# A planned graph-network kernel: the first batch's layer 0 chunk by chunk, first transfers ranked by need, its diagonal blocks on VectorE, and a new planned cost of a power

## The chip, the cores and the metric

One core of one Trainium2 chip. The metric is the device time of one execution in microseconds (us), over 32 batches. "Before" and "after" are the two kernels; each experiment was run on one chip together with runs of the kernel before, and is compared with those. A difference between runs of two sessions is marked as such; the kernel before had medians of 2319.06 to 2320.55 us in the sessions of the experiments.

## The reference

Four pre-normalized graph layers on x (32 batches of 512 nodes by 128 features), each with the batch's dense 512 by 512 adjacency:

```python
# layer 0: normalized adjacency with self loops
h = jnp.maximum(_layernorm(x, axis=-1), 0.0)
def _L0_gnn_ref(X, adj, W, b):
    XW = jnp.einsum('bnf,fo->bno', X, W)
    adj = adj + jnp.eye(adj.shape[1], dtype=adj.dtype)[None]
    d = jnp.sum(adj, axis=-1)
    r = d ** (-0.5)
    adj = adj * r[:, :, None] * r[:, None, :]
    y = jnp.einsum('bnm,bmo->bno', adj, XW) + b
    return jax.nn.leaky_relu(y, negative_slope=0.01)
x = x + _L0_gnn_ref(h, adj, ...)
# layers 1 to 3: layernorm, relu, then
#   1: two aggregations (adj and its transpose) of ELU features, tanh update
#   2: four inner layers, each with two aggregations by l2-normalized adjacency
#   3: one aggregation and a GRU-like gate
# ... each ends in x = x + layer(h, adj)
```

Every layer starts with a layernorm, and the l2 normalization needs inverse norms too, so each batch computes inverse square roots five times (four of them for the layernorms); here they are powers with exponent -0.5, done by GpSimd.

## The kernel before

The program is not written in the order in which it runs. Each operation is entered with an estimated cost, and a planner simulates the engines and fixes the order on each engine (and the buffer slots) before the program is built. Batches overlap: while TensorE works on one batch, the chains of the next are woven in between. Costs therefore change nothing on the chip by themselves; they change which instruction stands ahead of which.

Names in the views: v, sc and nb are the steps of the layernorm chain (variances, their power, the bias), h is its result; f is the tanh that ends an inner layer; blk is a transpose on VectorE, on the way of a tensor out to DRAM and back in another layout; f4r is such a turned tensor, read back from DRAM as turn_f4r; sd, rep and agg are operands of TensorE's products (ps_...). *Idle products* are products of the identity, put in where TensorE is planned to have nothing to do.

```python
PERIOD = 30.0
class Plan:
    SIGNAL = {"PE": 0.2, "DVE": 0.13, "ACT": 0.14, "POOL": 0.0, ...}
    RATE, ALONE, TRANSFER, ISSUE = 400.0, 175.0, 1.5, 0.45   # model of a transfer
    def op(self, engine, us, emit, reads=(), writes=(), kb=0.0, rank=None, later=0.0):
        ...
        if kb:
            o.us = max(self.ISSUE, kb / self.RATE)
            o.land = self.TRANSFER + kb / self.ALONE - o.us
    def order(self):
        ...
            due = o.batch * PERIOD if o.batch < B - 1 else (B - 2) * PERIOD + ENDING
            o.key = (due - o.tail + o.later if o.rank is None else o.rank - 1e6, i)
        ...  # events: each engine takes the ready operation with the lowest key
    def kept_warm(self, done, product, begin):
        ...  # where TensorE is planned idle for over SHORT us, n idle products are put in

def t_pow(n):                 # planned cost of a power over n columns
    return 0.9 + 0.1 * n

def normed(xin, out_tag, extra=None):          # layernorm and relu, every layer
    ... mv = moments(xin, v8)                  # VectorE
    if extra: extra(v8); n = 2 * NC            # layer 0: row sums of the adjacency too
    op("POOL", t_pow(n), lambda: nc.gpsimd.tensor_tensor(inv..., op=ALU.pow), ...)
    ... # layer 0: one VectorE multiply of two 4-column operands (sc)
    op("DVE", 0.08, ... nb = -mean * inv ...)
    for c in range(NC):
        op("ACT", t_act(D, 2), ... h = Relu(x * inv + nb) ...)

def degree(v8):                                # row sums, ScalarE
    for c in range(NC):
        op("ACT", 0.73, lambda c=c: nc.scalar.activation(
            sq.ap(), a.ap()[:, c, :], AF.Copy, accum_out=stat.ap()[:, c:c + 1]), ...)
hr, inv0 = normed(xt, "h", degree)

def own(k, n):                                 # diagonal blocks of aT plus identity
    nc.gpsimd.tensor_tensor(diag.ap()[:, k:k + n, :], blocks, ident..., op=ALU.add)
n = NC if b else 1                             # 4 of 128 columns first, then 1 of 512
```

## Time and profile before

Median of 3 runs: 2320.03 us.

The prediction below shows the page, the steady stretches and the head's timeline. The form whose time it takes for a row sum is VectorE's tensor_tensor of 128x512 f32, 687 to 689 ns in this trace (aT and a by rows, L739). One view also belongs here: what each engine waits for, summed over the run. First the head of TensorE's list in the kernel before (columns: total us, times, longest):

```profile
PE ps_agg L326 <- ACT f L768: 3.8, 5, 1.1
```

and the line of ScalarE's list that belongs to the layernorm chain:

```profile
ACT h L478 <- DVE nb L474: 144.1, 73, 8.2
```

TensorE waits for almost nothing. ScalarE waits 144 us for nb, the last VectorE step of a chain VectorE, GpSimd power, VectorE, ScalarE. That is harmless as long as what stands *behind* h in ScalarE's order is not needed yet. One such thing is f, the tanh that ends an inner layer and that TensorE needs for its next products.

### The profile page before, as it was taken

How to read it: one execution, taken by the hardware profiler on the slowest of the kernel's cores; microseconds unless marked ns; L12 is line 12 of the kernel's file. 1: busy time of each engine (PE TensorE's matmuls, PEld its weight loads, DVE VectorE, ACT ScalarE, POOL GpSimd, SP SyncE). 2: the span in 40 equal slices, each digit the busy share in tenths (PEclk: the TensorE clock that was granted, in tenths of full speed). 3: DMA queues.
4: the chain of work that ended last, by engine and by line, in shares of the span. 5: the costliest groups of instructions: out<-in, count | busy, mean ns of one | idle time of the engine just before them, and what ended most of it. 6: DMA issues, size and time to landing. Idle time of an engine off the chain costs nothing.

```text
span 2319.2 us, 28279 instructions
## 1 busy us (share of the span) xinstructions
PE 2301.0 (99%) x9682; PEld 1446.3 (62%) x9682; DVE 1530.8 (66%) x4132; ACT 946.4 (41%) x2018; POOL 262.6 (11%) x218
## 2 busy tenths in 40 slices
PE   9999999999999999999999999999999999999998
PEld 7656666666666566666666666666666666656665
DVE  5655666666667676676766676766766666767655
ACT  7323344334443344443344433444433444334412
POOL 3001101011111011010111101110101111101101
PEclk9999999999999999999999999999999999999999
DMA  7102332233222232222332322322223322223200
GB/s 261 46 10 64 105 94 75 81 101 107 76 91 82 82 109 81 87 79 86 105 100 83 91 82 82 109 81 88 78 86 105 107 76 91 82 82 105 77 6 27
DMA packets 133054, 200.82 MB, mean 87 GB/s; under 512 B 18992, under 2 KB 79920, under 8 KB 132912
## 3 DMA queue, kind: packets, MB, share of 16 engines
q1 hardware_dynamic: 132624, 198.90, 28.0%
q8 instruction: 76, 1.25, 0.2%
q14 instruction: 66, 0.54, 0.1%
q10 hardware_dynamic: 288, 0.13, 0.0%
HBM read 160.05 MB, written 38.93 MB: 86 GB/s over the span
## 4 chain that ended last, share of the span: by engine, by line
PE 91%; DMA 3%; DVE 3%; ACT 2%; POOL 1%; SPq 0%; issue 0%; DVEq 0%; ACTq 0%; POOLq 0%
PE ps_agg L326 61%; PE ps_seven L597 11%; PE ps_sd L326 9%; PE ps_upd L326 4%; PE ps_gate L326 2%; PE ps_msg L326 1%; DMA f4r<-turn_f4r 1%; PE ps_node L326 1%; PE ps_lin L326 1%; ACT h L478 1%; DMA turn_f4r<-blk 1%; POOL sc L466 1%; SPq L496 0%; ACT f L768 0%; DVE bn L450 0%
## 5 line engine op out<-in xcount | busy, mean ns | idle before, releaser
L326 PE MATMUL ps_agg<-aT,sd 128*128 128x512 f32 x1024 | 510.5, 594 | 0.1
L326 PE MATMUL ps_agg<-a,sd 128*128 128x512 f32 x1024 | 482.4, 592 | 0.0
L466 POOL TENSOR_TENSOR sc<-v,neg_half 128x4 f32<-128x4 f32 (+1 forms) x128 | 157.8, 1233 | 1638.6 <-DVE v L453 1361.8
L326 PEld LDWEIGHTS ps_agg<-a,sd 128*128 128x128 f32 x1024 | 184.6, 190 | 182.8 <-issue 178.4
L326 PE MATMUL ps_agg<-f,w_sb 128*128 128x512 f32 x448 | 229.6, 594 | 3.9 <-ACT f L768 3.8
L326 PEld LDWEIGHTS ps_agg<-aT,sd 128*128 128x128 f32 x1024 | 177.7, 191 | 83.0 <-issue 66.7
L326 PE MATMUL ps_sd<-w_sb,f 128*128 128x256 f32 x768 | 217.4, 380 | 0.5 <-ACT f L768 0.4
L478 ACT ACTIVATE h<-xr,nb,sc 128x128 f32<-128x128 f32 x384 | 158.2, 482 | 136.4 <-DVE nb L474 136.3
L597 PEld LDWEIGHTS ps_seven<-t_sb,s 128*128 128x128 f32 x1128 | 161.6, 191 | 78.1 <-issue 69.3
L326 PEld LDWEIGHTS ps_sd<-w_sb,f 128*128 128x128 f32 x768 | 136.6, 191 | 95.2 <-issue 76.5
L597 PE MATMUL ps_seven<-t_sb,s 128*128 128x128 f32 x1128 | 168.1, 275 | 0.0
L735 ACT COPY rows<-spaced 128x1024 f32<-128x1024 f32 x32 | 66.1, 2064 | 164.9 <-DMA spaced<-bounce 164.9
L326 PE MATMUL ps_agg<-aT,rep 128*128 128x512 f32 x256 | 131.3, 596 | 2.1 <-DVE rep L693 2.1
L326 PE MATMUL ps_agg<-a,rep 128*128 128x512 f32 x256 | 131.3, 596 | 0.0
L768 ACT ACTIVATE f<-ps_agg,cf_sb 128x512 f32<-128x512 f32 x128 | 87.2, 682 | 98.8 <-PE ps_agg L326 98.8
L326 PE MATMUL ps_agg<-aT,msg 128*128 128x512 f32 x256 | 124.9, 592 | 0.0
L487 DVE STREAM_TRANSPOSE blk<-f 128x512 f32<-128x512 f32 x29 | 20.6, 711 | 144.2 <-ACT f L768 144.2
L326 PE MATMUL ps_agg<-aT,h 128*128 128x256 f32 (+2 forms) x384 | 99.3, 381 | 0.2 <-ACT h L478 0.2
L597 PEld LDWEIGHTS ps_seven<-w_sb,f 128*128 128x128 f32 x512 | 75.9, 191 | 35.4 <-issue 27.7
L739 DVE TENSOR_TENSOR aT<-aT,rows 128x512 f32<-128x512 f32 x128 | 87.9, 687 | 14.7 <-PE ps_agg L326 14.6
L553 DVE TENSOR_TENSOR sd<-ps_sd,rf_sb 128x512 f32<-128x512 f32 x128 | 86.9, 679 | 15.5 <-PE ps_sd L326 15.4
L739 DVE TENSOR_TENSOR a<-a,rows 128x512 f32<-128x512 f32 x128 | 88.1, 689 | 13.6 <-PE ps_agg L326 13.5
(144 smaller groups left out, 3817.3 us busy)
## 6 DMA issues: line engine op xcount, KB each, us to landing
aT<-in_adjt SPq DMA_DIRECT2D x124, 512.0 KB, 5.2
a<-in_adj SPq DMA_DIRECT2D x62, 512.0 KB, 5.2
turn_turned<-blk SPq DMA_DIRECT2D x348, 64.0 KB, 1.8
turned<-turn_turned SPq DMA_DIRECT2D x87, 256.0 KB, 2.6
spaced<-bounce SPq DMA_DIRECT2D x32, 512.0 KB, 4.0
x<-in_x SPq DMA_DIRECT2D x32, 256.0 KB, 2.8
out<-xo SPq DMA_DIRECT2D x30, 256.0 KB, 2.0
turn_f4r<-blk SPq DMA_DIRECT2D x116, 64.0 KB, 1.8
```

The lines of the kernel that those rows point to most:

```text
L326: op("PE", t_mm(n), lambda: nc.tensor.matmul(out_of(ps.ap()), lhs(), rhs(), start=start, stop=stop), reads, [ps], later=later)
L466: op("POOL", t_pow(n), lambda: nc.gpsimd.tensor_tensor(inv.ap()[:, :n], v8.ap()[:, :n], neg_half[:, :n], op=ALU.pow), [v8, NH], [(inv, {0})])
L478: op("ACT", t_act(D, 2), lambda c=c: nc.scalar.activation(h.ap()[:, c, :], xin.ap()[:, c, :], AF.Relu, bias=nb.ap()[:, c:c + 1], scale=inv ...
L487: op("DVE", t_tt(N), lambda: nc.vector.transpose(blk.ap().rearrange("p b (c r) -> p c b r", c=NC), m.ap().rearrange("p c (b s) -> p c b s" ...
L553: op("DVE", t_tt(N), lambda ps=ps, h=h: nc.vector.tensor_add(sd.ap()[:, 2 * h:2 * h + 2, :], ps.ap().rearrange("p (j v) -> p j v", j=2), s ...
L597: op("PE", t_mm(D), lambda j=j: nc.tensor.matmul(ps.ap()[:, k * H + j * D:k * H + (j + 1) * D], lhs()[:, j * P:(j + 1) * P], rhs(), start= ...
L735: op("ACT", t_act(2 * N), lambda: nc.scalar.copy(rows.ap().rearrange("p s (c n) -> p (s c) n", c=NC), spaced.ap().rearrange("p n k -> p k ...
L739: op("DVE", t_tt(N), lambda m=m, c=c, s=s: nc.vector.tensor_mul(m.ap()[:, c, :], m.ap()[:, c, :], rows.ap()[:, s, :]), [(m, {c}), rows], [ ...
L768: op("ACT", t_act(N, 1), lambda ps=ps, i=i, f_new=f_new: nc.scalar.activation(f_new.ap(), ps.ap(), AF.Tanh, bias=cf_sb[:, i:i + 1]), [ps, ...
```

## The change

The intent: the layer-0 chain of the first batch shall follow the adjacency chunk by chunk, so that TensorE starts its first aggregation sooner. Four parts, cut to the core:

```diff
+OWN = 1
+FIRST = ["x0", "a0", "c", "raw0", "aT0", "w1", "r1", "raw2", "raw3"]
     def t_pow(n):
-        return 0.9 + 0.1 * n
+        return 0.35 + 0.157 * n
+    def first(name):
+        return FIRST.index(name) if name in FIRST else None
-        op("SP", 0.5, lambda: nc.sync.dma_start(c_sb, bcol), [], [CS], kb=9, rank=2)
+        op("SP", 0.5, lambda: nc.sync.dma_start(c_sb, bcol), [], [CS], kb=9, rank=first("c"))
 ... (the other transfers likewise)
+        def normed_by_chunk(xin, out_tag):
+            mv = moments(xin, v8)
+            op("POOL", t_pow(NC), ... pow of the 4 variances ...)
+            for c in range(NC):
+                op("DVE", t_tt(N), ... tensor_reduce(stat[:, c], a[:, c, :], AX.X, ALU.add) ...)
+                op("DVE", 0.08, ... v8 = stat + 1 ...)
+                op("POOL", t_pow(1), ... pow of one column ...)
+                op("DVE", 0.08, ... multiply the two inverses ...)
+                op("DVE", 0.08, ... nb ...)
+                op("ACT", t_act(D, 2), ... h of this chunk ...)
-        hr, inv0 = normed(xt, "h", degree)
+        hr, inv0 = normed_by_chunk(xt, "h") if b < 1 else normed(xt, "h", degree)
-            nc.gpsimd.tensor_tensor(diag..., op=ALU.add)
+            own_engine.tensor_tensor(diag..., op=ALU.add)
+        own_engine, own_name = (nc.vector, "DVE") if b < OWN else (nc.gpsimd, "POOL")
```

Three parts touch the first batch alone. The cost of a power touches the plan of all 32.

More of the change, by code (lines that the diff above doesn't have):

```diff
@@ L341, in setup @@
         op("POOL", 0.2, lambda: nc.gpsimd.memset(neg_half, -0.5), [], [NH])
-        first = W_L2[0][0]
+        first_l2 = W_L2[0][0]
         def spread(lo, hi, to=None):
@@ L351, in setup @@
             r_sb[:, :D], bass.AP(tensor=brow.tensor, offset=brow.offset, ap=[[0, P], [1, D]])), [], [(RS, {0})], kb=64)
-        op("SP", 0.5, lambda: nc.sync.dma_start(c_sb, bcol), [], [CS], kb=9, rank=2)
-        op("SP", 0.5, lambda: nc.sync.dma_start(w_sb[:, D:first], w[:, D:first]), [], [(W1, {1})], kb=(first - D) / 2, rank=5)
-        op("SP", 0.5, spread(D, R_L3_MSG), [], [(RS, {1})], kb=(R_L3_MSG - D) / 2, rank=5)
+        op("SP", 0.5, lambda: nc.sync.dma_start(c_sb, bcol), [], [CS], kb=9, rank=first("c"))
+        op("SP", 0.5, lambda: nc.sync.dma_start(w_sb[:, D:first_l2], w[:, D:first_l2]), [], [(W1, {1})], kb=(first_l2 - D) / 2, rank=first("w1"))
+        op("SP", 0.5, spread(D, R_L3_MSG), [], [(RS, {1})], kb=(R_L3_MSG - D) / 2, rank=first("r1"))
         op("SP", 0.5, spread(R_L3_MSG, R_COLS), [], [(RS, {2})], kb=(R_COLS - R_L3_MSG) / 2)
@@ L364, in setup @@
             op("SP", 0.5, lambda buf=buf, lo=lo, hi=hi: nc.sync.dma_start(
-                buf.ap().rearrange("p c n -> p (c n)")[:, :hi - lo], raw[:, lo:hi]), [], [buf], kb=(hi - lo) / 2, rank=3 if i == 0 else 6)
+                buf.ap().rearrange("p c n -> p (c n)")[:, :hi - lo], raw[:, lo:hi]), [], [buf], kb=(hi - lo) / 2, rank=first(f"raw{i}"))
             raws += [(buf, lo)] * (2 if i == 0 else 1)
-        op("SP", 0.5, lambda: nc.sync.dma_start(w_sb[:, W_L3_MSG:], w[:, first:]), [], [W3], kb=(W_COLS - W_L3_MSG) / 2)
+        op("SP", 0.5, lambda: nc.sync.dma_start(w_sb[:, W_L3_MSG:], w[:, first_l2:]), [], [W3], kb=(W_COLS - W_L3_MSG) / 2)
         def block(i, col):
@@ L435, in load @@
         def load(dst, src, kb, rank):
+            rank = first(f"{rank}{b}")
             n = NC // pieces
@@ L440, in load @@
                 op("SP", 0.4, lambda s=s: nc.sync.dma_start(dst.ap()[:, s, :], src[:, s, :]),
-                   [], [(dst, set(range(NC)[s]))], kb=kb / pieces, rank=None if b else rank)
-        op("SP", 0.4, lambda: nc.sync.dma_start(xt.ap(), x[b]), [], [xt], kb=256, rank=None if b else 0)
-        load(a, adj[b], 1024, 1)
-        load(aT, adjt[b], 1024, 4)
+                   [], [(dst, set(range(NC)[s]))], kb=kb / pieces, rank=rank)
+        op("SP", 0.4, lambda: nc.sync.dma_start(xt.ap(), x[b]), [], [xt], kb=256, rank=first(f"x{b}"))
+        load(a, adj[b], 1024, "a")
+        load(aT, adjt[b], 1024, "aT")
         def moments(xin, v8):
@@ L454, in moments @@
             return mv
+        def normed_by_chunk(xin, out_tag):
+            v8, inv, nb = buf("v8", (P, 2 * NC)), buf("sc", (P, 3 * NC)), buf("nb", (P, NC))
+            mv = moments(xin, v8)
+            op("POOL", t_pow(NC), lambda: nc.gpsimd.tensor_tensor(inv.ap()[:, :NC], v8.ap()[:, :NC], neg_half[:, :NC], op=ALU.pow),
+               [(v8, {0}), NH], [(inv, {0})])
+            h, stat = buf("s2", rows_shape, out_tag), buf("stat", (P, NC))
+            for c in range(NC):
+                at, mark = NC + c, 1 + c
+                op("DVE", t_tt(N), lambda c=c: nc.vector.tensor_reduce(stat.ap()[:, c:c + 1], a.ap()[:, c, :], AX.X, ALU.add),
+                   [(a, {c})], [(stat, {c})])
+                op("DVE", 0.08, lambda c=c, at=at: nc.vector.tensor_scalar_add(v8.ap()[:, at:at + 1], stat.ap()[:, c:c + 1], 1.0),
+                   [(stat, {c})], [(v8, {mark})])
+                op("POOL", t_pow(1), lambda at=at: nc.gpsimd.tensor_tensor(
+                    inv.ap()[:, at:at + 1], v8.ap()[:, at:at + 1], neg_half[:, :1], op=ALU.pow), [(v8, {mark}), NH], [(inv, {mark})])
+                op("DVE", 0.08, lambda c=c: nc.vector.tensor_mul(
+                    inv.ap()[:, 2 * NC + c:2 * NC + c + 1], inv.ap()[:, c:c + 1], inv.ap()[:, NC + c:NC + c + 1]),
+                   [(inv, {0, mark})], [(inv, {mark + NC})])
+                op("DVE", 0.08, lambda c=c: nc.vector.scalar_tensor_tensor(
+                    nb.ap()[:, c:c + 1], mv.ap()[:, c, 0:1], -1.0, inv.ap()[:, 2 * NC + c:2 * NC + c + 1], op0=ALU.mult, op1=ALU.mult),
+                   [mv, (inv, {mark + NC})], [(nb, {c})])
+                op("ACT", t_act(D, 2), lambda c=c: nc.scalar.activation(
+                    h.ap()[:, c, :], xin.ap()[:, c, :], AF.Relu, bias=nb.ap()[:, c:c + 1],
+                    scale=inv.ap()[:, 2 * NC + c:2 * NC + c + 1]), [xin, (nb, {c}), (inv, {mark + NC})], [(h, {c})])
+            return h, inv
         def normed(xin, out_tag, extra=None):
@@ L648, in own @@
             blocks = bass.AP(tensor=t.tensor, offset=t.offset + k * (N + P), ap=[list(t.ap[0]), [N + P, n], [1, P]])
-            nc.gpsimd.tensor_tensor(diag.ap()[:, k:k + n, :], blocks, ident[:, None, :].to_broadcast([P, n, P]), op=ALU.add)
+            own_engine.tensor_tensor(diag.ap()[:, k:k + n, :], blocks, ident[:, None, :].to_broadcast([P, n, P]), op=ALU.add)
         n = NC if b else 1
+        own_engine, own_name = (nc.vector, "DVE") if b < OWN else (nc.gpsimd, "POOL")
         for k in range(0, NC, n):
-            op("POOL", t_pool(n * P), lambda k=k, n=n: own(k, n), [(aT, set(range(k, k + n))), ID], [(diag, set(range(k, k + n)))])
+            op(own_name, t_tt(n * P) if b < OWN else t_pool(n * P), lambda k=k, n=n: own(k, n), [(aT, set(range(k, k + n))), ID], [(diag, set(range(k, k + n)))])
         psh = plan.bank("agg")
@@ L797, in program @@
         aT2 = buf("s8", (P, NC, N), "aT2")
-        load(aT2, adjt[b], 1024, None)
+        load(aT2, adjt[b], 1024, "again")
         aggregate(psa, msg, 0, aT2)
```

## The prediction

> **What bounds the kernel now.** I read the page first (busy shares, the 40 slices), then the idle products, busy time by stretch, and last the head's timeline and chain of waits.
>
> ```profile
> PE 2301.0 (99%) x9682; PEld 1446.3 (62%) x9682; DVE 1530.8 (66%) x4132; ACT 946.4 (41%) x2018; POOL 262.6 (11%) x218
> ...
> 0.00:14.00 14.00, 9.48 (x58) 9.29 (x58) 1.00 0.85 292
> 14.00:30.00 16.00, 4.87 (x40) 4.68 (x40) 1.00 0.95 357
> ...
> 400.00:1000.00 600.00, 597.20 (x2492) 372.80 (x2491) 404.13 (x1096) 248.61 (x524) 67.17 (x51) 1.00 0.30 90
> 1000.00:1600.00 600.00, 600.00 (x2508) 374.83 (x2508) 408.74 (x1089) 246.83 (x521) 63.46 (x50) 1.00 0.29 89
> 1600.00:2200.00 600.00, 599.78 (x2510) 375.50 (x2509) 402.61 (x1079) 253.29 (x534) 69.17 (x53) 1.00 0.30 90
> ```
>
> Line 1: TensorE is busy 99% of 2319.2 us. The next two are the idle products alone (products of the identity[...]): 9.5 us before 14 us and 4.9 us from 14 to 30. The last three are the steady state: 3.0 us lost in 1800. From about 62 us to 2280 us TensorE has no room, so whatever the head gains reaches the end nearly whole, and whatever the change does to the steady state can only cost or give what is lost there.
>
> So the prize is in the first 60 us. From the same views TensorE's time there is: nothing useful until the first fold product at 11.14; a hole of 0.95 us at 12.7 to 13.66; idle products of 3.2 us at 24.07 and 1.35 us at 28.46; holes of about 3 us between 32 and 36.5; half clock from 38 to 41, worth about 1.7 us; 0.8 us of idle products at 54.4. That is 11 us before the first useful product and about 11 after.
>
> ```profile
> 5.41 0.63 ACT L638 ACTIVATE sq<-a 128x512 f32<-128x512 f32 x1 [2.47 <-DMA a<-in_adj]
> ...
> 9.22 0.63 ACT L638 ACTIVATE sq<-a 128x512 f32<-128x512 f32 x1
> ...
> 10.23 1.65 POOL L466 TENSOR_TENSOR sc<-v,neg_half 128x8 f32<-128x8 f32 x1 [8.89 <-DVE v L640]
> 11.14 1.57 PE L326 MATMUL ps_fold<-raw 128*128 128x128 f32 x12 [0.27 <-DMA raw<-in_raw]
> 11.65 0.63 ACT L717 ACTIVATE sq<-aT 128x512 f32<-128x512 f32 x1 [1.71 <-DMA aT<-in_adjt]
> ...
> 13.03 1.63 ACT L478 ACTIVATE h<-x,nb,sc 128x128 f32<-128x128 f32 x4
> ...
> 13.66 0.46 PE L326 MATMUL ps_agg<-diag,h 128*128 128x128 f32 x2 [0.94 <-ACT h L478]
> ...
> 22.04 0.67 DVE L673 TENSOR_TENSOR xr<-x,y 128x512 f32<-128x512 f32 x1
> ...
> 26.59 1.65 ACT L478 ACTIVATE h<-xr,nb,sc 128x128 f32<-128x128 f32 x4 [0.62 <-DVE nb L474]
> ...
> 29.80 1.89 PE L326 MATMUL ps_sd<-w_sb,hT 128*128 128x256 f32 x8
> ```
>
> The reader is to see one serial chain: the four row sums on ScalarE end with the last chunk of the adjacency (10 us), one power over 8 columns on GpSimd, two small VectorE steps, then h from 13.03. The aggregation (ps_agg) runs 13.66 to 17.39 and the first product of layer 1 (ps_sd) stands at 29.80. The transposed chunks were there before: they land at about 11.6, 12.3, 12.9 and 13.55 (where the Square and the diagonal blocks start). The aggregation now waits for h, not for its data.
>
> [...] This trace has 687 to 689 ns for that form, so I take 0.69 us for one row sum (the trace has no tensor_reduce). [...] Here a 128x128 block costs GpSimd 455 ns and VectorE 280 (weight differences) to 349 ns (output sums): less than twice at this size. [...] after the thin stretch 34 to 36 the granted clock reads 0.50 from 38 to 41. [...] This trace moves 402 to 430 GB/s from 10 to 16 us[...].
>
> **The change part by part.** *Ranks by need.* Old ranks were x 0, adjacency 1, column biases 2, raw0 3, transposed 4, w1 and r1 5, raw2 and raw3 6; ties go by order of creation. The list gives the same order. Worth 0, and landings stay where they are.
>
> *Cost of a power in the plan* (0.9+0.1n to 0.35+0.157n): no instruction changes; 4 columns go from 1.3 to 0.98 us and 8 from 1.7 to 1.61 in the static schedule, for all 32 batches. The trace means are 1.09 and 1.66, so the new figures are as near as the old. It reshuffles orders everywhere; I allow +-1.5 us, as there are 5 to 6 us of loss from 62 to 2280.
>
> *Row sums by VectorE, chunk by chunk.* Removed: 4 activations with accumulator read (about 0.74 us each, 3.0 us of ScalarE), one 8-column power. Added: 4 reductions of 0.69, 12 small VectorE steps of 0.15, one power of 4 columns early (hidden: x lands at 3.7) and four of one column. From 4 columns at 1.01 us and 8 at 1.65, one column extrapolates to about 0.53 us (estimate). After a chunk has landed: reduction 0.69 + add 0.17 + hop 0.1 + power 0.53 + multiply 0.15 + bias 0.17 + hops 0.1 + h 0.48 = 2.4 us. The last chunk of a is there by 9.2, so h is complete at about 11.6 to 11.8 instead of 14.66. VectorE is nearly empty from 5 to 13, so the added 5 us there cost nothing.
>
> *Diagonal by VectorE.* 4 x 0.28 to 0.35 instead of 4 x 0.455; after the last landing at 13.55 it is ready at about 13.9 instead of 14.06.
>
> *On the path.* Both inputs of the aggregation now meet at the transposed chunks: start about 12.0 (11.6 + 0.3 + hop), 0.93 us a chunk as before (3.73/4), so the end is 12.0 + 3.7 = 15.6; the last chunk, landed at 13.55, does not hold it. That is 1.8 us before 17.39. The fold products that filled 11.14 to 12.7 move into later holes, so first useful product moves from 11.14 to 12 and the 0.95 hole goes: even. Further on two small stalls should fall: VectorE, in order, held xr from 21.28 to 22.04 for the normalization of batch 1's x, whose transfer landed at 21.8 (0.75 us); with the chain planned 2 us earlier xr stands ahead of it. And the nb step at 25.33 took 1.23 us instead of 0.17 beside GpSimd's 512-wide diagonal (up to 1 us, half counted). Sum at ps_sd: 1.8 + 0.75 + 0.5 = 3.0 us, taken from the 4.55 us of idle products ahead of it.
>
> Then rows: ScalarE stood at the copy of the inverse norms (31.14 to 33.2, after the bounce through DRAM), and rep had to wait behind it. The row-sum work gone lets the Squares end sooner than 19.7 and so the bounce. If rows goes earlier too, the 3 us of holes and the 1.7 us of half clock shrink; if not, part of the 3.0 is lost there. I take +1 on balance. Total: about 4 us, 2320.0 to **2316 us**.
>
> **The rivals.** (1) *The head is bound by transfers and the gain is given back at rows or at later loads*: for it, queues at 400 GB/s until 30 us and the bounce landing at 31.12, where ScalarE's order is fixed; against it, the bounce itself starts from the Squares, which move up. It makes 2319 to 2320. (2) *The clock drops*: if fewer idle products are planned and the first real one waits for a transposed chunk at 11.6, TensorE stands 1 to 2 us; a drop like that at 38 us would cost about 1.7 us and eat the aggregation's gain: 2318. Against it, the 0.95 us hole at 12.7 did no harm. (3) *The whole of the head closes*: holes at 24 to 36 and the half clock all go, 7 to 9 us: 2311 to 2313. (4) *The reshuffled schedule costs a hole or a longer tail* (the last 36 us has 8 us of holes and a fixed serial ending): 2321 to 2323.
>
> **Range and chances.** The cap is 11 us of 2320, 0.5%: no outcome I can build from this profile is near 2% (46 us) either way. Range **2311 to 2320.5** for 8 in 10: the low end is rival 3, the high end rival 1. Faster by over 2%: 0.005; within: 0.99; slower: 0.005 (a schedule gone wrong in all 32 batches).
>
> **What would show it.** In the changed kernel's timeline: four reductions of about 0.69 us, h complete before 12 us, ps_agg starting near 12.0 right after the first transposed chunk and ending near 15.6; landings of a and aT within 0.3 us of the old; ps_sd at about 26.8; idle products of 14 to 30 us down by 2 to 3 us; the stretches from 400 to 2200 as full as now. Wrong if ps_agg still starts after 13 (order on VectorE or ScalarE holds h), if rep still starts its product at 36 (rival 1), if the clock falls at 10 to 14 us (rival 2), or if the steady stretches lose more than 6 us.

## The result and the profile after

After: **2347.21 us** median (2344.16 to 2349.99, 5 runs), against 2319.75 (2319.23 to 2321.92, 5 runs) for before in the same session. The ratio is 1.0117 (95%: 1.0102 to 1.0131). A ratio here is the mean time of one kernel's fast runs over the mean of the other's in the same rounds, so not quite the ratio of the medians quoted. The kernel is 27 us slower; 2316 and its range up to 2320.5 were wrong, and so was the direction. It is still within 2%.

The head did what was meant. Timeline of the kernel after (columns: start, duration, engine, line, operation):

```profile
5.30 0.69 DVE L472 TENSOR_REDUCE stat<-a 128x1 f32<-128x512 f32 x1 [0.71 <-DMA a<-in_adj]
...
6.40 0.56 POOL L476 TENSOR_TENSOR sc<-v,neg_half 128x1 f32<-128x1 f32 x1 [5.05 <-DVE v L474]
...
9.60 1.90 ACT L484 ACTIVATE h<-x,nb,sc 128x128 f32<-128x128 f32 x4 [3.57 <-DVE nb L481]
...
11.24 0.29 DVE L682 TENSOR_TENSOR diag<-aT,ident 128x128 f32<-128x128 f32 x1 [0.27 <-DMA aT<-in_adjt]
...
11.68 0.46 PE L332 MATMUL ps_agg<-diag,h 128*128 128x128 f32 x2 [1.93 <-DVE diag L682]
```

A row sum takes 0.69 us, a one-column power 0.56, h is complete at 11.50, and the aggregation starts at 11.68 as soon as the first diagonal block is there, where it had stood at 13.66.

The loss is in the steady state. Busy time by stretch, kernel after (columns: stretch, its length, then busy us of TensorE, its weight loads, VectorE, ScalarE, GpSimd):

```profile
400.00:1000.00 600.00, 594.93 (x2478) 370.99 (x2476) 402.32 (x1087) 245.65 (x522) 65.38 (x51) 1.00 0.30 90
1000.00:1600.00 600.00, 592.36 (x2465) 369.21 (x2466) 406.83 (x1078) 240.91 (x508) 61.21 (x48) 1.00 0.29 86
1600.00:2200.00 600.00, 589.89 (x2455) 367.86 (x2454) 399.77 (x1054) 245.14 (x522) 65.49 (x51) 1.00 0.30 89
```

TensorE loses 5.1, 7.6 and 10.1 us, 22.8 in 1800, where it had lost 3.0. The clock is full (1.00) throughout. What TensorE waits for, kernel after:

```profile
PE ps_agg L332 <- ACT f L802: 18.1, 26, 1.9
PE ps_agg L332 <- DVE sd L586: 4.5, 12, 0.7
```

The wait for f has gone from 3.8 to 18.1 us. Why f is late is visible in one of the 26 places (timeline of the kernel after):

```profile
1356.06 0.71 DVE L520 STREAM_TRANSPOSE blk<-h 128x512 f32<-128x512 f32 x1 [0.28 <-ACT h L511]
...
1356.70 0.13 DVE L460 TENSOR_SCALAR v<-mv 128x4 f32<-128x4 f32 x1
...
1356.97 1.05 POOL L499 TENSOR_TENSOR sc<-v,neg_half 128x4 f32<-128x4 f32 x1 [3.77 <-DVE v L460]
...
1358.05 0.16 DVE L507 SCALAR_TENSOR_TENSOR nb<-mv,sc 128x4 f32<-128x4 f32 x1 [0.90 <-POOL sc L499]
...
1358.25 1.65 ACT L511 ACTIVATE h<-xr,nb,sc 128x128 f32<-128x128 f32 x4 [2.22 <-DVE nb L507]
...
1359.80 0.67 ACT L802 ACTIVATE f<-ps_agg,cf_sb 128x512 f32<-128x512 f32 x1
...
1360.52 1.13 PE L332 MATMUL ps_agg<-f,w_sb 128*128 128x512 f32 x2 [0.56 <-ACT f L802]
```

Read it upwards, from the last line. TensorE waits 0.56 us for f. f itself waited for no other engine: it has no bracket, it simply stood behind h on ScalarE. h waited 2.22 us for nb, and VectorE's nb waited 0.90 for the power. ScalarE stood idle for 2.22 us, holding f behind an instruction that could not start. Over the run, ScalarE waits 214 us for nb, against 144.

The first two lines show what the new order did. The same steps in the kernel before:

```profile
1347.10 0.16 DVE L453 TENSOR_SCALAR v<-mv 128x4 f32<-128x4 f32 x1
...
1347.51 0.70 DVE L487 STREAM_TRANSPOSE blk<-h 128x512 f32<-128x512 f32 x1
...
1348.49 0.16 DVE L474 SCALAR_TENSOR_TENSOR nb<-mv,sc 128x4 f32<-128x4 f32 x1 [0.28 <-POOL sc L466]
```

There v stood ahead of the transpose of 0.70 us, which VectorE then did while GpSimd computed the power; nb waited 0.28. In the kernel after the transpose stands ahead of v, so the power starts later, VectorE has little to do beside it, and nb waits 0.90. All 26 places are alike: nb waits 0.90 for a power of 1.04 to 1.11 us, and h waits 2.2 to 2.4. So are all 24 places of e1 (below); in e2 (below) and the kernel before, nb waits 0.28 and h 1.3 to 1.5.

The 26 waits are not all of one size. Twenty are of 0.26 to 0.76 us. The six longest, 1.2 to 1.9 us (8.8 of the 18.1), come every third batch from 1001 us on; there a second cause adds to the first (part 5).

Comparing the programs' instruction orders, which the planner fixes (no time is read from that), gave the first suspicion. The list of ranks alone changes no order on any engine, as predicted. The three parts for the first batch change no engine's order from the fourth batch on, but for a few places on ScalarE. The new cost of a power alone moves about half of TensorE's planned operations out of their old places (2407 of 4805 when the two planners are replayed), and it is the figure for 4 columns that does it: with the new figure for 8 columns alone TensorE's order is the old one.

### The profile page after: what moved, and what is told of

Same layout as the page of the kernel before. It is cut to its first block, busy times and chain, and to the rows that moved or that the text cites.

```text
span 2345.8 us, 28211 instructions
## 1 busy us (share of the span) xinstructions
PE 2306.2 (98%) x9658; PEld 1445.8 (62%) x9658; DVE 1542.6 (66%) x4149; ACT 940.0 (40%) x2010; POOL 256.6 (11%) x218
## 4 chain that ended last, share of the span: by engine, by line
PE 74%; DVE 8%; DMA 7%; ACT 7%; SPq 2%; POOL 2%; issue 1%; POOLq 0%; DVEq 0%; ACTq 0%
PE ps_agg L332 51%; PE ps_seven L630 8%; PE ps_sd L332 7%; PE ps_upd L332 4%; DMA spaced<-bounce 3%; ACT h L511 3%; PE ps_gate L332 2%; SPq L529 2%; ACT rows L769 2%; DVE blk L520 2%; POOL sc L499 1%; ACT f L802 1%; DMA f4r<-turn_f4r 1%; PE ps_msg L332 1%; PE ps_node L332 1%
## 5 line engine op out<-in xcount | busy, mean ns | idle before, releaser
L499 POOL TENSOR_TENSOR sc<-v,neg_half 128x4 f32<-128x4 f32 (+1 forms) x127 | 151.2, 1191 | 1664.4 <-DVE v L460 1306.7
L332 PE MATMUL ps_agg<-f,w_sb 128*128 128x512 f32 x448 | 231.4, 599 | 18.1 <-ACT f L802 18.1
L332 PEld LDWEIGHTS ps_agg<-aT,sd 128*128 128x128 f32 x1024 | 172.5, 191 | 78.6 <-issue 45.7
L332 PE MATMUL ps_agg<-aT,rep 128*128 128x512 f32 x256 | 126.4, 593 | 1.1 <-DVE rep L727 1.1
L671 ACT ACTIVATE sq<-a 128x512 f32<-128x512 f32 x124 | 77.6, 626 | 124.5 <-DMA a<-in_adj 122.8
L332 PE MATMUL ps_agg<-a,rep 128*128 128x512 f32 x256 | 126.0, 592 | 0.0
L520 DVE STREAM_TRANSPOSE blk<-h 128x512 f32<-128x512 f32 x87 | 61.8, 710 | 61.4 <-ACT h L511 60.9
L332 PEld LDWEIGHTS ps_agg<-f,w_sb 128*128 128x128 f32 x448 | 75.6, 191 | 42.4 <-ACT f L802 23.0
```

The costliest lines, as they stand in the source:

```text
L332: op("PE", t_mm(n), lambda: nc.tensor.matmul(out_of(ps.ap()), lhs(), rhs(), start=start, stop=stop), reads, [ps], later=later)
L499: op("POOL", t_pow(n), lambda: nc.gpsimd.tensor_tensor(inv.ap()[:, :n], v8.ap()[:, :n], neg_half[:, :n], op=ALU.pow), [v8, NH], [(inv, {0})])
L520: op("DVE", t_tt(N), lambda: nc.vector.transpose(blk.ap().rearrange("p b (c r) -> p c b r", c=NC), m.ap().rearrange("p c (b s) -> p c b s" ...
L671: op("ACT", 0.73, lambda c=c: nc.scalar.activation(sq.ap(), a.ap()[:, c, :], AF.Copy, accum_out=stat.ap()[:, c:c + 1]), [(a, {c})], [sq, ( ...
```

## The experiments

### 1. The cost of a power alone, and everything else alone

Theory: the planned cost of a power is the cause. Rivals: the new head, or just any reshuffling of a finely balanced order.

e1 (before with the new cost only):
```diff
-        return 0.9 + 0.1 * n
+        return 0.35 + 0.157 * n
```

> The kernel before with only the planner's cost of a power changed (0.35+0.157n for 0.9+0.1n); no instruction is added or removed, only the static orders change. Theory A (the smaller cost takes away slack that the norm chain needs; ScalarE then stands in order behind h and its tanh f comes late): about 2340 to 2350 us, TensorE waiting for ACT f some 15 to 20 us in all. Rival B (the chunk-wise head shifts the phase of the pipeline and that costs the 27 us): 2319 to 2322, like before. Rival C (any reordering lands somewhere at random): anything from 2316 to 2350.

e2 (after with the old cost):
```diff
-        return 0.35 + 0.157 * n
+        return 0.9 + 0.1 * n
```

> The changed kernel with the old cost of a power; chunk-wise chain, ranks and VectorE diagonal stay. Theory A: the steady state of before returns, so 2315 to 2320 us, and TensorE's wait for ACT f in all falls from 18 to about 4 us. Rival B: 2340 to 2350 as in the changed kernel. Rival C: unknown.

e3 (after, the new cost for the first batch only):
```diff
-        return 0.35 + 0.157 * n
+        return 0.35 + 0.157 * n if plan.batch < 1 else 0.9 + 0.1 * n
```

> The changed kernel with the new cost of a power in the first batch alone (and the old one for batches 1 to 31). Theory A: like the run above, 2314 to 2320 us, a microsecond or so below it if the better estimate helps the head. Rival B: 2340 to 2350.

e4 (before, with another perturbation of the plan that has nothing to do with the change):
```diff
-PERIOD = 30.0
+PERIOD = 30.3
```

> The kernel before with the planner's period 30.3 for 30.0: every priority of later batches shifts, the cost of a power stays the old one, no instruction changes. Theory A: the slack is kept, so within 5 us of before (2316 to 2326). Rival C (the steady state of before was luck and any reshuffle costs some 20 us): 2335 or more.

Measured, before 2319.18 in the same session: e1 **2341.94** (ratio 1.0101), e2 2325.67 (1.0029), e3 2324.42 (1.0020), e4 2325.57 (1.0029). So the cost function, which changes no instruction, makes 22.8 us by itself. The rest of the change also loses, 5 to 6.5 us, against the expectation of 2314 to 2320 for e2 and e3, and so does an arbitrary other order. The two losses add to 29.3, about what the whole change has (27.5). e1 shows the same signature as after, TensorE's list and ScalarE's:

```profile
PE ps_agg L326 <- ACT f L768: 13.0, 24, 1.7
PE ps_agg L326 <- DVE sd L553: 5.2, 12, 0.7
```
```profile
ACT h L478 <- DVE nb L474: 206.5, 62, 8.2
```

Between the traces of e1 and before (2339.1 and 2319.2 us), TensorE's holes account for 13.6 of the 19.9 us. Part of the rest is in its busy time (2307.3 against 2301.0): from 400 to 2200 us a product of 512 columns that follows a hole takes 697 ns, another 592 (medians), and e1 has 34 such, before 4.

What is left open after this: whether the power's time is really what makes e1's order slow, and where e2's 6.5 us come from.

### 2. The order of e1 with a quick power

Theory: in e1's order, h is planned to come just after the power; the power's real duration plus hand-overs that the plan lacks make it late. If the power is made much quicker with the order left alone, the loss must go. Rival: the order is bad for another reason. The power was exchanged for a multiply by 0.01 (relative error 0.79), planned at the same cost. e6 is the same edit in the kernel before, as control. Their outputs are wrong, which doesn't matter for the times.

```diff
-nc.gpsimd.memset(neg_half, -0.5)
+nc.gpsimd.memset(neg_half, 0.01)
-    ... neg_half[:, :n], op=ALU.pow)
+    ... neg_half[:, :n], op=ALU.mult)
```

> The program of the run with only the planner's cost changed (2341.9 us), order of every engine the same, but each power on GpSimd computed as a multiplication by 0.01, which is quicker; the result is wrong on purpose. Theory A (the order is good only if the power ends when the plan says; h then holds up f on ScalarE): with the power well under the planned 0.98 us the waits of TensorE for ACT f (13 us) and for DVE sd (5 us) go, 2318 to 2325 us. Rival D (the new order is worse by itself, by transfers or bank turns, whatever the power takes): 2336 or more.

> Control: the kernel before with the same multiplication in place of the power, wrong result on purpose. Theory A: before has slack for the power nearly everywhere (3.8 us of waits for ACT f), so it gains little, 2314 to 2319 us. If it gains 15 us or more, the multiplication helps by another way than the order and the run above tells nothing.

Measured: e5 **2317.33**, e6 2315.37, before 2320.09. The GpSimd step falls from a mean of 1185 ns to 232 in e1's order, and the wait for f from 13.0 us to 2.0:

```profile
PE ps_agg L326 <- ACT f L768: 2.0, 2, 1.1
```

The same edit is worth 24.6 us in e1's order (over two sessions) and 4.7 in before's. The slowness of e1 is therefore the power's real time meeting an order that leaves it no room. The old figure of 1.3 us for 4 columns was too long by 0.2 us against the measured 1.09, and I read that excess as what paid for hand-overs that the plan does not know. One of these, from a power's end to nb, is 0.03 us in the traces of before and after (medians) and 0.0 in the plan; the sum of them was not measured. The new figure of 0.98 us is too short by 0.11 (by 0.05 against e1's own mean of 1.03). That it is the side of the error that counts is not shown: no run planned the power at its measured time, or longer than 1.3 us.

### 3. Which part of the rest loses

Before, with the chunk-by-chunk chain alone (e7), and with the first diagonal on VectorE alone (e11), both with the old cost and with the list of ranks:

```diff
 # e7, against e2
-OWN = 1
+OWN = 0
 # e11, against e2
-hr, inv0 = normed_by_chunk(xt, "h") if b < 1 else normed(xt, "h", degree)
+hr, inv0 = normed(xt, "h", degree)
```

> The kernel before with the chunk-wise chain alone (old planned cost of a power, GpSimd diagonal). From batch 3 on the planned order of TensorE, VectorE, GpSimd and the transfers is that of before. Theory E (the head's gain is real, about 4 us up to batch 5, and is lost later to landings that come later than planned): ahead of before by 3 to 4 us at the sixth batch, in all 2318 to 2327 us. Rival F (the head's gain was never there): not ahead at the sixth batch.

> The kernel before with the first diagonal block by VectorE alone (old planned cost of a power, row sums by ScalarE). TensorE's order and its number of instructions are those of before, and h comes no sooner, so: 2318.5 to 2321 us, the same as before. More than 3 us either way would be against theory G, as the fetches stay where they are.

Measured: e7 2322.90 (ratio 1.0012, 0.9997 to 1.0027), e11 2319.19 against 2319.06 (1.0001, 0.9993 to 1.0010). The diagonal alone, with the ranks, is worth nothing. The chunk-by-chunk chain ends the first batches sooner and then loses what it gained and more: e2's sixth batch reaches its layer-1 update 4.4 us before that of the kernel before (375.54 against 379.94 in the traces; e7's is 2.8 us ahead, 3 to 4 were expected), but e2 ends 6.5 us later. From the fourth batch on, its TensorE order is identical. An unchanged order that loses time must lose it to something that is not in the order.

### 4. A remedy that only moved the wait

If missing slack is the matter, more slack for every transfer in the plan should help. e2 with:

```diff
-    RATE, ALONE, TRANSFER, ISSUE = 400.0, 175.0, 1.5, 0.45
+    RATE, ALONE, TRANSFER, ISSUE = 400.0, 175.0, 1.7, 0.45
```

> The changed kernel with the old planned cost of a power (2325.7 us) and with every transfer planned to land 0.2 us later (1.7 us of fixed time for 1.5). No instruction changes. Theory E: the order then leaves room for late landings of the turned features, TensorE's wait for ACT f falls from 10 us to under 4, 2312 to 2319 us. Rival C (each reordering lands at random): no better than 2322.

Measured: 2347.07 us (before 2320.09; ratio 1.0117), a clear miss. The wait for f did fall, but another took its place. TensorE's list, e8:

```profile
PE ps_agg L332 <- DVE sd L586: 23.2, 28, 1.0
PE ps_agg L332 <- ACT f L802: 4.4, 7, 0.9
```

One of the 28 places (timeline of e8):

```profile
1041.59 1.69 POOL L682 TENSOR_TENSOR diag<-aT,ident 128x512 f32<-128x512 f32 x1
...
1042.08 1.23 DVE L504 TENSOR_TENSOR sc<-sc 128x4 f32<-128x4 f32 x1
...
1043.23 0.68 DVE L586 TENSOR_TENSOR sd<-ps_sd,rf_sb 128x512 f32<-128x512 f32 x1
...
1043.96 0.70 PE L332 MATMUL ps_agg<-aT,sd 128*128 128x512 f32 x1 [0.86 <-DVE sd L586]
```

A VectorE multiply of 4 columns, otherwise 0.15 us, takes 1.23. GpSimd's add ends at 1041.59 + 1.69 = 1043.28, the multiply at 1042.08 + 1.23 = 1043.31: it ends 0.03 us after GpSimd's add. What holds it is not in the trace; that it ends with the add is. In e2 the same two never met: its 31 multiplies have 0.15 to 0.28 us. In e8, 27 of 31 are over 1 us, each of them ends 0.02 us after a GpSimd add, and 25 of the 28 waits for sd follow one within 2.5 us.

The kernel before has one long meeting of this kind, which the prediction had read in its head: nb at 25.33, 1.23 us instead of 0.17, which ends at 26.56 beside a GpSimd add that ends at 26.54. Whether e8 loses by this was tested later (part 6).

### 5. What e2 loses: TensorE's instruction fetch beside a read

In e2, every third batch (213 us apart) from 566 to 1423 us the wait for f is 0.8 to 1.6 us, and the kernels derived from it have such batches too. The chain to it starts at f4r, a 256 KB read of turned features, which lands late: some 5 us after its issue instead of 3.4. The DMA queues at those moments hold one more thing: a fetch of instructions, taken to be TensorE's own. There are 76 in a run, of 16,384 bytes each, about every 30.5 us; 7 such intervals are 213 us, three batches of 71. So a fetch that meets the read meets it again every third batch. The profile gives these fetches a queue of their own, of the kind "instruction", and does not name the engine. Two things speak for TensorE: in the traces of before and after, its products and weight loads between one fetch and the next are 252 on average (202 to 308 in the single intervals of before, 218 to 290 in those of after), and the fetches move when idle products are taken out of its list (e10 below: from 2.9 us before the read near 987 us to 2.1 us after it). The cost does not lie on TensorE (the kernel before loses 0.0 us from 1000 to 1600, with 20 fetches), but on the read next to it.

I took each f4r read between 480 and 2130 us in the traces of eleven kernels of the old slack (before, after, e2, e3, e7, e9 to e14; 263 reads) and sorted them by where the nearest fetch starts, counted from the issue of the read:

| fetch starts, us after the read's issue | reads | issue to the add of f4r, median us | range |
|---|---|---|---|
| -16 to -3.4 | 99 | 3.42 | 2.78 to 4.17 |
| -3.4 to 1 | 15 | 3.43 | 2.71 to 3.91 |
| **1 to 3.1** | 35 | **4.83** | 3.82 to 5.31 |
| 3.1 to 16 | 114 | 3.43 | 2.91 to 4.08 |

The bounds of the bold row were chosen after looking: the expectations of e9 and e10 still have the harm begin before the read's issue. All sixteen kernels of the old slack give the same picture (41 reads in that row with a median of 4.80, the other rows at 3.42 to 3.52). The second row hides a cost. Where the fetch starts some 3 us before the read's issue, as at 560, 774 and 987 us in the kernel before, it meets the writes that the read has to follow: there the read is issued 4.1 to 4.2 us after the first write, elsewhere in that trace from 480 us on 3.2 to 3.6.

If the fetch goes by the number of TensorE's instructions, a few idle products more or fewer in the head move all later fetches against the work, by some 0.12 us an instruction (an estimate: 30.5 us by 252). (One product of the program is two products and two loads in the profile: six fewer in e10 are 12 products fewer there.) That can be tested in both directions: take five out of e3 (should win), and six out of the kernel before (should lose).

```diff
 # e9: e3 with left = 5; e10: before with left = 6 (idle products at 24 to 30 us)
+        left = 5
                     n = int(min(gap, cold) / self.COLD + max(gap - cold - 0.1, 0.0) / self.WARM)
+                    if not cold:
+                        dropped = min(n, left, 3)
+                        n, left = n - dropped, left - dropped
```

> The run with the new cost in the first batch alone (2324.4 us) less five of the eight idle products that stand between 24 and 29 us; orders, buffers and useful instructions are the same. Theory G (the steady loss comes from TensorE's instruction fetch[...], which in every third batch falls within -3.4 to +3 us of the issue of the turned features' read and makes them land 1 to 2 us late): 20 instructions fewer move every later fetch some 2.3 us on, out of that stretch; TensorE's waits for ACT f fall from 5.6 to under 2 us in all, 2315 to 2320 us. Rival H (the landings are late because of which buffers or which moment the head leaves behind, not because of the fetch): 2323 to 2326.

> The kernel before less six of its twenty idle products between 24 and 30 us, nothing else. Theory G: the fetch that lies 2.9 to 4.2 us ahead of that read in every third batch, mostly just harmless, moves 2.8 us on, to 0 to 1.4 us ahead of it: nearly every third batch up to the end loses 0.8 to 1 us where only four did; 2322 to 2326 us. Rival H: 2319 to 2321, like before.

Measured, before 2319.06: e9 **2319.17** (0.9999), 5.2 us better than e3; e10 **2324.90** (1.0024), 5.8 us worse than the kernel it was made from. Taking *work* of no use out of the old kernel made it slower. The waits for f, e9 then e10:

```profile
PE ps_agg L336 <- ACT f L806: 2.2, 5, 0.6
```
```profile
PE ps_agg L330 <- ACT f L772: 8.4, 10, 1.4
```

In e10's trace the fetch starts 2.5, 2.1 and 2.2 us after the reads at 772, 987 and 1201 us, which then reach the add in 5.0, 4.8 and 4.7 us. The time was as expected, the place was not: 0 to 1.4 us *before* the reads, in nearly every third batch, was expected. Against the kernel before the fetch moved by 5.0 to 6.0 us at these three reads, where 24 instructions (12 products and 12 loads) at 0.12 us make 2.9.

This also says what moved the fetch in e2. The profile counts 9682 products in before and 9670 in e2, whose head has room for fewer idle products, and 9670 in e10. With the same count, e2 and e10 have the fetch at nearly the same places, 2.8, 2.4, 2.4 and 2.5, 2.1, 2.2 us after the reads near 770, 985 and 1200 us; in the kernel before it starts 2.9, 2.9 and 3.8 us ahead of them.

Next, more at once. In e2, part of the first 26 idle products was replaced by half as many of twice the width: 12 by 6 (e12), 18 by 9 (e13), all 26 by 13 (e14). The profile counts 9658, 9652 and 9644 products, and as many loads, against 9670 in e2.

```diff
 # e12; e13 with 9 and 18, e14 with 13 and 26
-        for _ in range(n):
+        for _ in range(6 if n == 26 else 0):
+            nc.tensor.matmul(ps[:, :2 * P]..., ident, ident[:, None, :].to_broadcast([P, 2, P]), start=True, stop=True)
+        for _ in range(n - 12 if n == 26 else n):
             nc.tensor.matmul(ps[:, :P], ident, ident, start=True, stop=True)
```

> The changed kernel with the old planned cost of a power (2325.7 us), in which twelve of the first 26 idle products are replaced by six of double width: TensorE's busy time is the same, but it has 24 instructions fewer. Orders, buffers and useful work are the same. Theory G: the fetch moves 2.8 us on, from 2.1-2.8 us after the issue of the turned features' read in every third batch to 4.9-5.6 us, where it did no harm in the other runs; the clock is kept, so the head's lead of some 4 us at the sixth batch lasts to the end: 2313 to 2318 us, faster than before. Rival H: 2324 to 2327, as without it.

> The kernel of e2, with 18 of the first 26 idle products replaced by 9 wide ones of 256 columns each, so TensorE has 36 instructions fewer (a matrix load and a product each) and the fetches of its instructions come later against the work: at 30.5 us per 255 instructions that is 0.12 us each, 4.3 us in all, less the 1 to 2 us by which e12 drifted back. Theory (the loss of e2 is the fetch 1 to 3 us after the issue of the f4r read): the fetch stands at +4 to +7 us from that issue, f4r reaches xr in 3.4 us in every third batch, TensorE's wait for f falls from 10.0 to under 5 us and the time is 2316 to 2320. Rival (the loss sits in the order that the new head leaves, whatever the fetch does): 2323 to 2326, f wait still 8 to 10 us.

> As e13 with all 26 as 13 wide ones, 52 TensorE instructions fewer, 6.2 us by the same reckoning. Fetch theory: at +6 to +9 us, clear of the read and of the turn's write by more than in e13; f wait under 5 us, time 2316 to 2320. Rival (order): 2323 to 2326. If e13 wins and e14 loses, or the other way, the fetch theory stands only if the trace shows the fetch back within 1 to 3.1 us after the read's issue in the one that lost.

Measured: e12 2323.47 (before 2319.66; 1.0018), e13 2322.72 (before 2320.55; 1.0002), e14 **2318.80** (before 2320.55; 0.9990, 0.9984 to 0.9997). Only e14 does what was expected of all three. (e13 is level with before by the ratio, which pairs runs of the same rounds, and 2.2 us slower by the medians.) The order after the head is that of e2 in all of them, so "the loss sits in the order" is ruled out. The traces say why e12 and e13 fell short. At the reads of every third batch from 555 us on, the fetch starts

- e2: 2.1, 2.8, 2.4, 2.4, 2.3 us after the read's issue (reads take 4.6 to 5.3 us), then 3.1 to 3.3 us before it (3.0 to 3.3 us),
- e12: 4.0, 3.3, then 1.8, 2.4, 2.5, 1.8, 2.3, 2.2 (3.6 to 3.9 us, then 4.3 to 5.0),
- e13: 3.7, 3.7, 3.2, 4.2, 4.0, then 1.9, 2.3, 2.4 (3.3 to 4.1 us, then 4.4 to 5.0),
- e14: 4.2, 3.6, 3.3, 3.4, 3.6, 3.6, 3.3, 3.3 (3.2 to 4.0 us throughout).

The loss follows the place of the fetch in each single batch. What was wrong in the expectations of e12 and e13 is how far the fetch moves and whether it stays there. Two reads, e2 then e14, in 4 us from shortly before the issue (the first line is the busy share of the DMA engines in 40 slices, tenths; then the read with its us to landing):

```profile
DMA  3089466995999999951997699779998421400001
...
f4r<-turn_f4r SPq DMA_DIRECT2D x1, 256.0 KB, 4.9
```
```profile
DMA  4649779699699901341549799977472110000080
...
f4r<-turn_f4r SPq DMA_DIRECT2D x1, 256.0 KB, 3.4
```

In e14 the read has ended and the fetch stands alone, the 8 at the far right. In e2 it falls into the busy stretch, and the read takes 1.5 us longer. The single packets of the trace show most of why. A fetch is one packet, of 0.94 us here (median of the run 1.06). The read is 128 packets of 2 KB with 16 end marks, so 8 packets for each mark. In e2 fifteen of the marks are there at 1414.16 us, the sixteenth at 1415.60; and the last 8 packets start at 1414.41, when the fetch (1413.48 to 1414.42) ends, and take 1.2 us. So a sixteenth of the read stands behind the fetch, and the read is done with its last part. In 27 of the 35 reads of the bold row the last 8 packets start within 0.02 us of the fetch's end.

### 6. The collision of e8, and slack after all

e8 with the diagonal adds of all batches on VectorE, so that GpSimd has no wide add left (e15), and the same edit in e2 as control (e16):

```diff
-OWN = 1
+OWN = B
```

> The kernel of e8 (2347.1 us, TensorE waits 23.2 us for sd) with the diagonal adds of all batches on VectorE, so GpSimd has no wide add left that could run beside VectorE's small multiply. Theory (the 1.23 us multiply beside GpSimd's 512-wide add made sd late once a batch): the multiply is 0.15 to 0.2 us again, the sd wait falls to under 8 us and the time to 2317 to 2328. Rival (the wider slack gives an order in which sd is late by itself): sd wait stays over 15 us and the time over 2338.

> Control for e15: the kernel of e2 (2325.7 us) with the diagonal adds of all batches on VectorE and the old slack. VectorE takes on some 31 x 0.7 us more and stays near 67% busy; I expect 2320 to 2328, so that e15 against e8 tells of the collision and not of a gain that any plan has from it. If e16 falls by 20 us against e2, the reading of e15 falls with it.

Measured, before 2320.55: e15 **2318.56** (0.9987, 0.9980 to 0.9995), e16 2324.53 (1.0011). Against e8 and e2, measured in other sessions, the edit gains 28.5 us in e8's plan and 1.1 in e2's. The small multiply, e8 then e15 (groups of instructions: count, total us, mean ns, idle time before):

```profile
L504 DVE TENSOR_TENSOR sc<-sc 128x4 f32<-128x4 f32 x31 | 33.8, 1091 | 2.1 <-POOL sc L499 2.1
```
```profile
L504 DVE TENSOR_TENSOR sc<-sc 128x4 f32<-128x4 f32 x31 | 4.9, 157 | 1.8 <-POOL sc L499 1.8
```

and what TensorE waits for in e15:

```profile
PE ps_agg L332 <- ACT f L802: 5.2, 7, 1.0
...
PE ps_agg L332 <- DVE sd L586: 0.7, 2, 0.4
```

So e8's loss was the meeting of the multiply with GpSimd's add (the edit changes the order too, but the multiply's own mean fell from 1091 to 157 ns), and the extra slack itself is good: e15 and e16 differ in nothing else, in one session, and e15 is 6.0 us faster. In e15 some reads of f4r still take 4.8 to 5.3 us beside a fetch, and the wait for f is half of e2's 10.0.

### 7. Everything together, and the old head under the same plan

e17 is e15 with e14's wide idle products. e18 is e15 with the old head:

```diff
 # e18, against e15
-hr, inv0 = normed_by_chunk(xt, "h") if b < 1 else normed(xt, "h", degree)
+hr, inv0 = normed(xt, "h", degree)
```

> e15 (2318.6 us) and e14 (2318.8 us) put together: slack of 0.2 us a transfer, diagonal of all batches on VectorE, all 26 first idle products as 13 wide ones. If the two losses of e2 add up, the 4.7 us of every-third-batch loss that e15 still has (f4r reaches xr in 4.8 to 5.3 us at four places) goes too: 2314 to 2317, the first version clearly before the old kernel. If slack already hides the fetch, nothing is added: 2318 to 2320.

> The old head (row sums by ScalarE, one power of 8 columns) with the ranks list, the slack of 1.7 and the diagonal of all batches on VectorE. If the new head is worth its 4 us wherever the order has slack: 2320 to 2323, 2 to 4 us over e15. If the gain of e15 came from slack and diagonal alone and the head adds nothing: 2317 to 2319, as e15.

Measured, before 2319.36 (33 runs): e17 **2317.00** (21 runs; 0.9991, 0.9984 to 0.9997), e18 2319.81 (13 runs; 0.9999, 0.9991 to 1.0008), between the two ranges that were expected of it. e17 is faster than both kernels, by 2 us over before and 30 over after (two sessions). It is the best correct version found, but e15 (0.9987) is the same within the intervals, so adding the two remedies is not shown to give more than one. In e17 the fetch still starts 2.0 to 2.8 us after some reads, which take 4.5 to 5.3 us: other orders, other phase. Against e18, the new head is worth 2.8 us of medians, 1.9 by the ratios; but e17 has the wide idle products too. e15, which differs from e18 in the head alone, is 2.8 us better by the ratios, over two sessions. In e18 as well the fetch stands 2.0 to 2.3 us after the read at five places, so 2 to 3 us is the head and whatever the place of the fetch adds.

| kernel | us | beside before | ratio |
|---|---|---|---|
| after | 2347.21 | 2319.75 | 1.0117 |
| e1 cost of a power alone | 2341.94 | 2319.18 | 1.0101 |
| e2 all but that | 2325.67 | 2319.18 | 1.0029 |
| e5 e1's order, quick power (wrong values) | 2317.33 | 2320.09 | 0.9985 |
| e6 control of e5 (wrong values) | 2315.37 | 2320.09 | 0.9978 |
| e14 e2, fetch moved | 2318.80 | 2320.55 | 0.9990 |
| e15 e2, slack, no GpSimd add | 2318.56 | 2320.55 | 0.9987 |
| e17 both | 2317.00 | 2319.36 | 0.9991 |

## Why the prediction was wrong

**The step that failed: "Cost of a power in the plan".** The prediction had the mechanism's first half (no instruction changes, orders are reshuffled everywhere) and allowed "+-1.5 us", because the new figures "are as near as the old" to the trace. Measured alone it is +22.8 us (e1). Nearness was the wrong test. The old 1.3 us for 4 columns erred on the long side of 1.09, the new 0.98 on the short side. With the new figure the planner put a transpose of 0.7 us ahead of v on VectorE, in 26 batches; nb then waits 0.90 us for the power instead of 0.28, and h, which stands ahead of f on ScalarE, is late. e5 shows that the power's real time is what hurts in that order.

**"Whatever the head gains reaches the end nearly whole"** failed too, by the second term: with the old cost the kernel still loses 6.5 us (e2). The new head has fewer idle products, and that moved TensorE's instruction fetches onto the f4r read of every third batch. e9, e10 and e14 show it from both sides. The kernel after has both losses: from 989 us on its fetch starts 1.7 to 2.5 us after the read of every third batch. The "3.0 us lost in 1800" of the kernel before was partly luck: in its own trace the fetch starts 2.3 us after the read at 345 us and that read takes 4.8, and at later ones it stays outside the bad 1 to 3.1 us (where it starts just before the read, it meets the writes ahead of it instead: TensorE waits 0.8 to 1.1 us for f there); e10 takes six idle products out and loses 5.8.

**Right: the head.** Reductions at 0.69, one-column power 0.56 (predicted 0.53), h complete at 11.50 (11.6 to 11.8), diagonal 0.29 on VectorE, aggregation from 11.68 (12.0), ranks without effect. **Rival 2, the clock**, occurred in the kernel after: TensorE stood 1.93 us before its first aggregation product, and the clock read 0.5 from 13.0 to 16.5 us, so the aggregation ended at 17.09, not 15.6. The nb step that was to be free of GpSimd's add took 1.24 us again, and ps_sd stood at 28.80. In e14, whose clock held until 34 us and whose nb took 0.16, the aggregation ends at 15.62 and ps_sd stands at 26.67, against 15.6 and 26.8 predicted. The gain of the head, "about 4 us", is 2 to 3 at the end where the order has slack (e15 and e17 against e18). One reading behind rival 1 was off: the queues moved 303 to 341 GB/s from 20 to 30 us, not 400.

**Rival 4** ("the reshuffled schedule costs a hole") was the right one, mis-sized tenfold at 1 to 3 us, and the last check named the place where it would show: steady stretches that lose more than 6 us. They lost 22.8. The cap that the range was built on ("no outcome I can build from this profile is near 2%") counted the holes that were there to be won, and not those that a reordering can open: 32 batches, one or two waits of 0.7 us each, are already 22 to 45 us (an estimate from the 26 waits for f of 0.7 us on average in the kernel after).

**Open:** how the place of the fetch shifts with the number of removed instructions (e12 and e13 drift back after some batches, e14 does not); what e4's other order loses its 6.4 us to (its wait for f is 4.6 us, and no f4r read after 480 us takes over 4.0 us from issue to add); and whether a planned power between 0.98 and 1.3 us, or over 1.3, would have kept the time. A replay of the planner gives yet other orders at 1.09, 1.2 and 1.5 us, and none of these was run.

## What to carry to other kernels

In a statically ordered kernel, an estimated duration also decides what stands in front of what, and can act as a safety margin. Before making one "more accurate", look at what stands behind the waiting instruction on its in-order engine, and test the estimate alone; that the side on which it errs matters is likely here, but not tested. If two kernels have the same order and differ in time, look at what is in no order: here instruction fetches beside a transfer (a read's use 4.83 us after its issue instead of 3.42) and a small VectorE step beside a wide GpSimd add (1.23 us instead of 0.15). A part that costs or gains a few tenths of a percent can only be judged against a control with the same disturbance.

## Hardware behaviour that the traces showed

- Instruction fetch: a fetch of 16 KB was one packet of some 1.0 us. With some 20 of them in 600 us TensorE lost 0.0 us (before, 1000 to 1600), but a fetch that starts 1 to 3.1 us after the issue of a 256 KB read made the read's use come 4.83 us after issue instead of 3.42 (medians of 35 and 99 reads).
- TensorE's clock: in the 20 heads traced here, it fell to half for 3.4 us during or soon after TensorE's hole ahead of its first aggregation product where that hole was of 2.5 to 2.9 us (e3, e9, e15, e16: four of four), in two of five where it was of 1.84 to 2.04 us (after and e13 yes; e2, e8 and e14 no), and in none of eleven where it was of 0.3 to 1.5 us.
- A power on GpSimd took 0.56 us for 1 column (after), 1.09 for 4 and 1.66 for 8 (means, before); a multiply in its place 0.23 and 0.27 (means of 4 and 8 columns together, e5 and e6).
- A multiply of 4 columns on VectorE took 1.23 us instead of 0.15 beside a 512-wide GpSimd add (e8, at 1042 us); 27 of the 31 were over 1 us.
